# FFN gate and up as a seven-product block scheme, with the results kept in DRAM and the down products at the end

## The chip, the cores and the metric

The kernel runs on one core of one Trainium2 chip. The metric is the device time of one execution in microseconds (us), given as the median of three runs. The engines are TensorE (PE in the profile, with PEld for its weight loads), VectorE (DVE), ScalarE (ACT), GpSimd (POOL) and SyncE (SP), which here only issues DMAs. Each engine works through its own queue in order.

## The reference, cut to what matters

The input x is (16, 256, 512): 16 batches, 256 channels, 512 positions. The first half is a cross attention with 16 heads of 16 channels, whose queries come from the layer norm of x and whose keys and values come from `ctx`. The second half is an FFN over the last axis, with 1376 inner columns. Its weights are given as indices into a table of 16 values. All numbers are float32.

```python
x = x + xattn(layernorm(x), ctx, mask, mask, Wq, bq, Wk, bk, Wv, bv)

def ffn(x, lut, gate_idx, up_idx, down_idx):        # x: (16, 256, 512)
    gate = einsum('bsh,oh->bso', x, lut[gate_idx])  # (1376, 512) weights
    up   = einsum('bsh,oh->bso', x, lut[up_idx])
    h    = silu(gate) * up
    return einsum('bsh,oh->bso', h, lut[down_idx])  # (512, 1376) weights

x = x + ffn(layernorm(x), lut, gate_idx, up_idx, down_idx)
```

## The kernel before, in words

**Units of work.** The 16x256 rows of x make 32 row tiles of 128 rows by 512 columns, and four row tiles make a row block, so there are 8 blocks n = 0 to 7. The 1376 inner columns make 11 strips o of 128 columns (the last has 96). The 512 columns of x are four parts h of 128, the contraction steps of a matmul.

**Order.** The schedule is written out by hand (`tc.manual_schedule()`), so each engine's queue has the order in which the Python emits its instructions. The attention comes first, as 256 steps over (head group, key part). In each step TensorE makes the scores twice, in two layouts: `pa` (L458), which VectorE reduces to a row maximum (`nm`, L474, two reductions per step), and `pb` (L466), which ScalarE turns into exponentials (`pt`, L478). `pa` runs AHEAD = 7 steps before `pb`. The tables `lumps` and `after` hold what else is emitted at a step: projections, `apply_v`, sums, DMAs.

**Row tiles after the attention.** `finish_rows(k)` makes row tile k on GpSimd and SP stores it to DRAM (`x2_d[k]`, L554). Later `load_x2(k)` (L168) loads it, `stats2(k)` takes mean and variance on VectorE (`bn_f`, L98, L99), `rstd2` makes the reciprocal deviations (ScalarE square root L103, then VectorE L104, L105), `norm2(k)` (L181) normalizes, and `turn2(k)` transposes with four small matmuls (L192) and copies the result to `xT` with ScalarE (L193). For the first FIRST = 3 blocks this is done within the attention's last steps; for the later blocks it is done between the FFN's products (`preparing`).

**Weights.** Nothing is gathered: `look_up` turns a piece of indices into table values with 19 VectorE instructions (4 bits, L122 and L126; 8 leaves, L136; 7 joins by `copy_predicated`, L140). Gate and up (`wg`, `wu`) come in 32 pieces of 128x344; down (`wd`) comes in 11 pieces of 128x512. The first EARLY = 24 pieces are made during the attention, two instructions per step or one in a busy step. The others are made in the FFN by `fill`, which emits a given number of such instructions. SP loads the indices of a piece (`idx`, L634, and `idx_d`).

**The FFN.** `gate_up(n, o)` makes eight matmuls (four for gate, four for up, L715) of one block and strip into two PSUM banks of the pool `ps_a`, then ScalarE's silu (L720) and VectorE's product (`ht`, L722). `down(n)` makes, for each of four row tiles, 11 matmuls over the strips into one bank of `ps_b` (L731), adds the row tile (L736) and stores the output (L738). For blocks 0 to 2 all `gate_up` come first, strip by strip, with 11 `fill` instructions after each, and then three `down`; from block 3 on, each block has its 11 `gate_up`, with the next block's preparation between them, and then its `down`. The pool `ps_b` has four banks; `ps_a` has two buffers of two banks.

**SP.** SP issues all loads and stores of the attention's later steps and of the FFN in order. A store waits on SP for the engine that makes its data, and what is behind it waits as well.

A float32 matmul of the program is two records in the profile.

Of the kernel before, what the change touches and what calls it, by code (L numbers as in the profile page):

```python
# [19 lines left out]
def kernel(  # L20
# [88 lines left out]
    def look_up(pool, dst, it, name):  # L109


        rows, n = it.shape
        v = nc.vector

        def new(tag):
            return pool.tile([P, n], I32, tag=tag, name=f"{tag}_{name}")[:rows]

        m, ops = [], []

        def low():  # L120
            m.append(new("b0"))
            v.tensor_scalar(m[0], it, 31, 31, ALU.logical_shift_left, ALU.arith_shift_right)  # L122

        def bit(i):
            m.append(new(f"b{i}"))
            v.tensor_scalar(m[i], it, 1 << i, None, ALU.bitwise_and)  # L126

        ops.append(low)
        for i in range(1, 4):
            ops.append(lambda i=i: bit(i))  # L130
        d = dst.bitcast(I32)
        got = {}

        def leaf(k, to):
            a, c = lut_x[:rows, k : k + 1], lut_i[:rows, 2 * k : 2 * k + 1]
            v.tensor_scalar(to, m[0], a, c, ALU.bitwise_and, ALU.bitwise_xor)  # L136
            got[k] = to

        def join(level, k, k2):
            v.copy_predicated(got[k], m[level], got[k2])  # L140

        ops.append(lambda: leaf(0, d))
        ops.append(lambda: leaf(1, new("ta")))
        ops.append(lambda: join(1, 0, 1))
        ops.append(lambda: leaf(2, new("tb")))
        ops.append(lambda: leaf(3, new("ta")))
        ops.append(lambda: join(1, 2, 3))
        ops.append(lambda: join(2, 0, 2))
        ops.append(lambda: leaf(4, new("tb")))
        ops.append(lambda: leaf(5, new("ta")))  # L150
        ops.append(lambda: join(1, 4, 5))
        ops.append(lambda: leaf(6, new("tc")))
        ops.append(lambda: leaf(7, new("ta")))
        ops.append(lambda: join(1, 6, 7))
        ops.append(lambda: join(2, 4, 6))
        ops.append(lambda: join(3, 0, 4))
        return ops
# [4 lines left out]
    rstds = cpool.tile([P, NK], F32, tag="rstds", name="rstds")  # L162
    nmrs = cpool.tile([P, NK], F32, tag="nmrs", name="nmrs")
    x2s, xns = {}, {}

    def load_x2(k):
        x2s[k] = rpool.tile([P, T], F32, tag="x2", name=f"x2t_{k}", bufs=4)
# [17 lines left out]
    def turn2(k):  # L185
        n, t = divmod(k, 4)
        if t == 0:
            xTs[n] = xpool.tile([P, NH, 4 * P], F32, tag="xT", name=f"xT_{n}")
        pt = ps_b.tile([P, 512], F32, tag="b", name=f"pt_{k}")
        xn = xns.pop(k)  # L190
        for h in range(NH):
            nc.tensor.transpose(pt[:, h * P : (h + 1) * P], xn[:, h * P : (h + 1) * P], ident)  # L192
        nc.scalar.copy(xTs[n][:, :, t * P : (t + 1) * P], pt.rearrange("p (h r) -> p h r", r=P))  # L193


    with ExitStack() as att:
# [43 lines left out]
        def rstd1_of(lo, hi):  # L240
            at = slice(lo * NCC, hi * NCC)
            row_rstd(mv1[:, at, :], rstd1[:, at], nmr1[:, at])
# [366 lines left out]
                after[stats_at[b] - 3].append(lambda b=b: load_xs(b))  # L609
            after[stats_at[b]].append(lambda b=b: stats1(b))  # L610
        for lo, hi in ((1, 2), (2, 6), (6, B)):
            after[stats_at[hi - 1]].append(lambda lo=lo, hi=hi: rstd1_of(lo, hi))
        after[-8] += [fill_rows, lambda: (load_xs(1), load_b(1), load_piece(lp, 0))]
        after[-7].append(lambda: set_ones(0))
        after[-4].append(lambda: set_ones(1))
# [9 lines left out]
            for w, idx in ((wg, gate_idxT), (wu, up_idxT))  # L625
            for h in range(NH)
        ]
        EARLY = 24
        its = {}

        def load_piece(pool, i):
# [18 lines left out]
        early = lookups(lp, 0, EARLY)  # L650
        busy = {s for s in stats_at.values()} | {4 * u - 3 for u in range(NU)}

        NT = 4 * FIRST
        turns = NSTEP - 2 * NT
        for i in range(NT):
            after[turns - 5 - 3 * (NT - i)].append(lambda i=i: load_x2(i))
            after[turns - 3 - 3 * (NT - i)].append(lambda i=i: stats2(i))
            busy.add(turns - 3 - 3 * (NT - i))
            after[turns - 3 + 2 * i].append(lambda i=i: load_x2(i))
            after[turns + 2 * i].append(lambda i=i: norm2(i))  # L660
            lumps[turns + 1 + 2 * i].append(lambda i=i: turn2(i))
        after[turns - 4].append(lambda: rstd2(0, FIRST))
        for s in range(min(min(after), min(lumps)), NSTEP + 2):
            sa = s + AHEAD if 0 <= s + AHEAD < NSTEP else None
            sb = s if 0 <= s < NSTEP else None
# [4 lines left out]
            for fn in after.pop(s, ()):  # L670
                fn()
            if s >= 0:
                n = 0 if s in stats_at.values() else 1 if s in busy else 2
                for _ in range(n + (3 if sa is None else 0)):
                    next(early, None)
        for _ in early:
# [7 lines left out]
            last += after[s]  # L684


    with ExitStack() as ffn:
        wd_pool = ffn.enter_context(tc.tile_pool(name="wd", bufs=1))
        lp = ffn.enter_context(tc.tile_pool(name="lookup2", bufs=1))
        f1 = ffn.enter_context(tc.tile_pool(name="ffn1", bufs=1))  # L690

        wd = wd_pool.tile([P, NO, T], F32, tag="wd", name="wd")
        nblocks = NK // 4

        def rows_of(o):
            return min(P, INTER - o * P)

        def lookups_d():
            for o in range(NO):
                rows = rows_of(o)  # L700
                it = lp.tile([P, T], I32, tag="idx", name=f"idx_d{o}", bufs=2)
                nc.sync.dma_start(it[:rows], down_idxT[o * P : o * P + rows, :])
                for op in look_up(lp, wd[:rows, o, :], it[:rows], f"d{o}"):
                    op()
                    yield

        hts = {n: [] for n in range(nblocks)}

        def gate_up(n, o):
            rows = rows_of(o)  # L710
            at = slice(o * P, o * P + rows)
            ps = ps_a.tile([P, 2, 512], F32, tag="a", name=f"pgu_{n}_{o}")
# [5 lines left out]
                    )  # L718
            sg = rpool.tile([P, 4 * P], F32, tag="us0", name=f"sg_{n}_{o}", bufs=5)
            nc.scalar.activation(sg[:rows], ps[:rows, 0, :], AF.Silu)  # L720
            ht = f1.tile([P, 4 * P], F32, tag="ht", name=f"ht_{n}_{o}", bufs=FIRST * NO + 1)
            nc.vector.tensor_tensor(ht[:rows], sg[:rows], ps[:rows, 1, :], ALU.mult)  # L722
            hts[n].append((ht, rows))

        def down(n):
            hs = hts.pop(n)
            for t in range(4):
                xr = load_x2(4 * n + t)
                po = ps_b.tile([P, 512], F32, tag="b", name=f"po_{n}_{t}")
                for o, (ht, rows) in enumerate(hs):  # L730
                    nc.tensor.matmul(  # L731
                        po, ht[:rows, t * P : (t + 1) * P], wd[:rows, o, :],
                        start=(o == 0), stop=(o == NO - 1),
                    )
                ob = rpool.tile([P, T], F32, tag=("rb", "xr")[t % 2], name=f"ob_{n}_{t}", bufs=1)
                nc.vector.tensor_tensor(ob, po, xr, ALU.add)  # L736
                b, o = divmod(4 * n + t, NCC)
                nc.sync.dma_start(out[b, o * P : (o + 1) * P, :], ob)  # L738

        def preparing(n):  # L740

            k = 4 * n

            def at(i):
                if n >= nblocks:
                    return
                if i == 0:
                    for t in range(4):
                        load_x2(k + t)
                elif i == 1:  # L750
                    for t in range(4):
                        stats2(k + t)
                    rstd2(n, n + 1)
                    load_x2(k)
                elif i <= 9:
                    t = (i - 2) // 2
                    if i % 2:
                        turn2(k + t)
                    else:
                        norm2(k + t)  # L760
                        if t < 3:
                            load_x2(k + t + 1)

            return at

        late = lookups(lp, EARLY, len(pieces))
        late_d = lookups_d()

        def fill(n):
            for _ in range(n):  # L770
                if next(late, 1) == 1:
                    next(late_d, None)

        for o in range(NO):
            for n in range(FIRST):
                gate_up(n, o)
                if (o, n) == (0, 0):
                    for fn in last:
                        fn()
                fill(11)  # L780
        for _ in late:
            pass
        for _ in late_d:
            pass
        for n in range(FIRST):
            xTs.pop(n)
        prep = preparing(FIRST)
        for n in range(FIRST):
            down(n)
            for i in range(4 * n, 4 * n + 4):  # L790
                prep(i)
        for n in range(FIRST, nblocks):
            prep = preparing(n + 1)
            for o in range(NO):
                gate_up(n, o)
                prep(o)
            xTs.pop(n)
            down(n)


# [44 lines left out]
```

## Time and profile before

| | |
|---|---|
| median of 3 runs | 1978.93 us (1978.54 to 1982.69) |
| profiled execution, its time | 1980.16 us |
| profiled execution, its span | 1978.4 us |
| mean granted TensorE clock | 0.987 |
| PE busy | 1913.9 us (97%) |
| DVE busy | 1202.9 us (61%) |
| ACT busy | 767.9 us (39%) |
| POOL busy | 442.2 us (22%) |
| gate and up matmuls, L715 (two weights) | 318.5 + 316.5 us busy, 1408 records |
| down matmuls, L731 | 306.5 us busy, 704 records |
| first gate_up record | at 1029.07 us |
| end of the last down product | at 1974.36 us |

The span is the time from the first to the last instruction of the profiled execution. The page's groups give, for a line of the kernel, an engine and a tile, the busy time, the mean of one instruction in ns, and the idle time of the engine just before, with who ended it. The page's slices cut the span into 40 equal parts of 49.5 us. The chain of waits goes back from the last instruction to what released it at each step; it lists start, length, engine, tile and line. The timeline lists start, length, engine, line and operation, and in brackets the idle time before it and what ended that. `out<-in` names the tile written and the tiles read.

### The profile page before, as it was taken

The numbers are of one execution on the slowest core, as the hardware profiler recorded it, in microseconds if no ns is written. First come the engines' busy times: TensorE is split into PE (matmuls) and PEld (weight loads), VectorE is DVE, ScalarE is ACT, GpSimd is POOL, SyncE is SP. The second block draws the span as 40 slices with busy tenths as digits, with TensorE's granted clock in tenths as the row PEclk, the third lists the DMA queues.
The fourth block names the chain that finished last, engine by engine and source line by source line (L and its number), as shares of the span: only waits on it lengthen the run. The fifth ranks groups of instructions, "written<-read, shape, count | busy, mean of one in ns | idle before, by whom it ended". The sixth has DMA issues, their size and how long they took to land.

```text
span 1978.4 us, 23940 instructions
## 1 busy us (share of the span) xinstructions
PE 1913.9 (97%) x9030; PEld 788.8 (40%) x9030; DVE 1202.9 (61%) x1779; ACT 767.9 (39%) x1427; POOL 442.2 (22%) x511
## 2 busy tenths in 40 slices
PE   9999999999999999988998999989999999999999
PEld 4333333333333333333333444434444444444443
DVE  6898999999999998877996799710111101011000
ACT  2776776777777776656660000000110101011000
POOL 5444445444444444333320000000000000000000
PEclk9999999999999999989999999989999999999999
DMA  5454333443434434433321000021101001010101
GB/s 179 138 155 142 111 99 106 126 117 113 121 94 115 125 116 122 122 104 100 108 76 38 18 22 22 23 73 63 64 0 61 24 32 53 22 64 0 42 0 38
DMA packets 96676, 155.69 MB, mean 79 GB/s; under 512 B 20260, under 2 KB 25256, under 8 KB 96560
## 3 DMA queue, kind: packets, MB, share of 16 engines
q1 hardware_dynamic: 92288, 151.11, 25.2%
q0 software_dynamic: 3168, 1.86, 0.4%
q8 instruction: 71, 1.16, 0.2%
q10 hardware_dynamic: 1104, 1.19, 0.2%
q14 instruction: 45, 0.37, 0.1%
HBM read 113.29 MB, written 35.55 MB: 75 GB/s over the span
## 4 chain that ended last, share of the span: by engine, by line
PE 82%; DMA 5%; DVE 5%; ACT 3%; issue 2%; SPq 2%; POOL 1%; POOLq 0%; DVEq 0%; ACTq 0%
PE pgu L715 30%; PE po L731 15%; PE pa L458 12%; PE pv L497 9%; PE pb L466 7%; PE pv L422 3%; ACT pt L478 3%; PE pk L390 2%; PE pq L390 2%; DVE nm L474 2%; DMA x2t<-x 2%; DMA xs<-in_x_dram 1%; DMA qp<-qd 1%; DMA rb<-rd 1%; PE pt L192 1%
## 5 line engine op out<-in xcount | busy, mean ns | idle before, releaser
L474 DVE TENSOR_REDUCE nm<-pa 128x2 f32<-128x1024 f32 x512 | 601.9, 1217 | 74.8 <-PE pb L466 70.2
L478 ACT ACTIVATE pt<-pb 128x512 f32<-128x512 f32 x1024 | 530.8, 601 | 150.3 <-PE pb L466 145.9
L458 PE MATMUL pa<-kp,qp 32*128 32x512 f32 x2048 | 522.9, 623 | 20.5 <-DVE nm L474 17.7
L466 PE MATMUL pb<-qp,kp 32*128 32x512 f32 x2048 | 521.4, 624 | 0.1
L715 PE MATMUL pgu<-xT,wg 128*128 128x512 f32 (+1 forms) x704 | 318.5, 595 | 7.9 <-DVE ht L722 7.3
L715 PE MATMUL pgu<-xT,wu 128*128 128x512 f32 (+1 forms) x704 | 316.5, 592 | 0.0
L720 ACT ACTIVATE sg<-pgu 128x512 f32<-128x512 f32 (+1 forms) x88 | 52.5, 597 | 672.0 <-PE pgu L715 665.7
L731 PE MATMUL po<-wd,ht 128*128 128x512 f32 (+1 forms) x704 | 306.5, 597 | 0.0
L722 DVE TENSOR_TENSOR ht<-sg,pgu 128x512 f32<-128x512 f32 (+1 forms) x88 | 60.4, 686 | 350.5 <-ACT sg L720 350.4
L458 PEld LDWEIGHTS pa<-kp,qp 32*128 32x128 f32 x2048 | 182.1, 186 | 223.8 <-DVE nm L474 163.8
L497 PE MATMUL pv<-pt,va 128*32 128x512 f32 x2048 | 249.7, 606 | 2.3 <-ACT pt L478 2.3
L466 PEld LDWEIGHTS pb<-qp,kp 32*128 32x128 f32 x2048 | 202.1, 185 | 76.5 <-issue 49.1
L731 PEld LDWEIGHTS po<-wd,ht 128*128 128x128 f32 (+1 forms) x704 | 134.9, 192 | 169.6 <-issue 168.4
L715 PEld LDWEIGHTS pgu<-xT,wu 128*128 128x128 f32 (+1 forms) x704 | 132.0, 188 | 170.1 <-issue 170.1
L715 PEld LDWEIGHTS pgu<-xT,wg 128*128 128x128 f32 (+1 forms) x704 | 131.2, 188 | 171.7 <-issue 158.8
L736 DVE TENSOR_TENSOR ob<-po,x2t 128x512 f32<-128x512 f32 x32 | 22.1, 692 | 277.4 <-PE po L731 277.4
L497 PEld LDWEIGHTS pv<-pt,va 128*32 128x32 f32 x2048 | 54.3, 110 | 178.8 <-ACT pt L478 88.9
L502 ACT COPY us<-pv 128x512 f32<-128x512 f32 x128 | 75.0, 586 | 94.9 <-PE pv L497 94.9
L486 POOL DMA_DIRECT2D qp<-mx x64 | 38.5, 602 | 322.7 <-DVE mx L485 163.6
L509 POOL TENSOR_TENSOR us<-us,us 128x512 f32<-128x512 f32 x64 | 81.4, 1272 | 16.7 <-ACT us L502 16.6
L422 PE MATMUL pv<-wv,ctx 128*128 128x256 f32 x256 | 73.4, 411 | 7.6 <-ACT pt L478 0.4
L433 POOL TENSOR_SCALAR va<-vt,cols 128x128 f32<-128x128 f32 x128 | 76.0, 600 | 6.6
(108 smaller groups left out, 1254.4 us busy)
## 6 DMA issues: line engine op xcount, KB each, us to landing
x2t<-x SPq DMA_DIRECT2D x96, 256.0 KB
kp<-kd SPq DMA_DIRECT2D x62, 256.0 KB
qp<-qd SPq DMA_DIRECT2D x62, 256.0 KB
rb<-rd SPq DMA_DIRECT2D x32, 256.0 KB
xr<-in_x_dram SPq DMA_DIRECT2D x32, 256.0 KB
x<-xr SPq DMA_DIRECT2D x32, 256.0 KB
out_dram<-ob SPq DMA_DIRECT2D x32, 256.0 KB
kd<-natk SPq DMA_DIRECT2D x31, 256.0 KB
```

Of the source, the lines that this page charges most:

```text
L390: nc.tensor.matmul(ps, w[:, o, oc * P : (oc + 1) * P], src_t[:, o, :], start=(o == 0), stop=(o == NCC - 1),)
L422: nc.tensor.matmul(ps[:, :C], cx[:, o, c * P : (c + 1) * P], wv[:, o, :], start=(o == 0), stop=(o == NCC - 1),)
L433: nc.gpsimd.tensor_scalar(a4[:, e, :, 16 * e : 16 * e + 16], v4[:, e], m, None, ALU.mult)
L458: nc.tensor.matmul(pa[:, jj, :], qps[ua % 4][at, ca * P : (ca + 1) * P], kps[ua % 4][at, :], start=True, stop=True,)
L466: nc.tensor.matmul(pb, kps[ub % 4][at, cb * P : (cb + 1) * P], qps[ub % 4][at, :], start=True, stop=True,)
L474: nc.vector.tensor_reduce(nms[ua][:, 2 * half : 2 * half + 2, ca], pa, AX.X, ALU.max, negate=True)
L478: nc.scalar.activation(pts[sb][:, j, :], pb, AF.Exp)
L497: nc.tensor.matmul(ps[32 * j : 32 * j + 32, :], vas[b % 2][:, c, 8 * oc + 2 * j + e, :], pt[:, j, :], start=(i == 0), stop=(i == 1),)
L502: nc.scalar.copy(us[u, half], ps)
L509: nc.gpsimd.tensor_tensor(a, a, b, ALU.add)
L715: nc.tensor.matmul(ps[:rows, i, :], w[:, h, at], xTs[n][:, h, :], start=(h == 0), stop=(h == NH - 1),)
L731: nc.tensor.matmul(po, ht[:rows, t * P : (t + 1) * P], wd[:rows, o, :], start=(o == 0), stop=(o == NO - 1),)
```

## The change

**Seven products.** For two row blocks 2p and 2p+1 and one strip o, gate and up with both halves of the contraction form a product of two 2x2 block matrices: the weights are (a11 a12; a21 a22), with gate in the first row and up in the second and two parts h in each block; the activations are (b11 b12; b21 b22), with one column for each row block. The old way takes eight block products of two matmuls. The new `unit(p, o)` takes seven, by Winograd's form, and so needs sums of the weights (`combine_w`: S1, S2, S4 in the new tile `sw`, S3 in the place of a21) and of the activations (`combine_x`: the new tile `xe`, and T1 in the place of b12). Both are VectorE instructions, the sums of the weights of 512 to 768 elements per partition, those of the activations of 1024. Each product goes to one bank of `ps_b`. ScalarE copies the first; VectorE adds the others up with seven instructions that each read one PSUM bank; ScalarE makes silu twice; GpSimd multiplies twice; SP stores both results to DRAM (`hds`).

**Order of the FFN.** Strip 0 of blocks 0 to 3 is made by `gate_up` as before. Then come 42 units in the list `order`: strips 1 to 7 for the pairs 0 and 1 in turn, strips 8 to 10 of each of them, then pairs 2 and 3 with all 11 strips. A unit emits 14 `fill` instructions, between its adds. `hooks` puts the statistics of tiles 16 to 31 into units 0 to 8, one `rstd2` for all four later blocks into unit 9, and the normalizing and turning of blocks 4 and 5, and 6 and 7, into units 17 to 19 and 22 to 24.

**Down.** All eight `down` come after the last unit. The h of block 0 is loaded back at unit (3, 2); each `down(n)` first loads the row tiles and issues the load of block n+1 (2.8 MB, two buffers), whose memory is that of the sums and lookups, closed just before.

**Lookups.** EARLY is 22. Pieces 22 to 31 and the down weights are made in `between`, together with `combine_w`. Down pieces are halves of 256 columns, each with its own index load at its start.

**Attention.** Statistics are taken of 16 row tiles, not 12, and their loads stand four steps ahead, not two; `rstd2(0, 4)` stands two steps earlier. Block 3 is turned at the start of the FFN, into its own pool `x3pool` and through `ps_a`. `rstd1_of` of the later batches stands one step later. From step 179 on one lookup instruction is emitted per step, not two.

```diff
-        EARLY = 24
+        EARLY = 22
...
+        for i in range(16):
+            after[turns - 9 - 3 * (16 - i)].append(lambda i=i: load_x2(i))
+            after[turns - 5 - 3 * (16 - i)].append(lambda i=i: stats2(i))
...
-            after[turns - 5 - 3 * (NT - i)].append(lambda i=i: load_x2(i))
-            after[turns - 3 - 3 * (NT - i)].append(lambda i=i: stats2(i))
...
-        after[turns - 4].append(lambda: rstd2(0, FIRST))
+        after[turns - 6].append(lambda: rstd2(0, 4))
...
-                n = 0 if s in stats_at.values() else 1 if s in busy else 2
+                n = 0 if s in stats_at.values() else 1 if s in busy or s > turns - 54 else 2
...
+        def combine_w(lo, hi):
+            at = slice(lo, hi)
+            s1, s2, s4 = (sw[:, i, :, at] for i in range(3))
+            yield v.tensor_tensor(s1, a21[:, :, at], a22[:, :, at], ALU.add)
+            yield v.tensor_tensor(s2, s1, a11[:, :, at], ALU.subtract)
+            yield v.tensor_tensor(a21[:, :, at], a11[:, :, at], a21[:, :, at], ALU.subtract)
+            yield v.tensor_tensor(s4, a12[:, :, at], s2, ALU.subtract)
...
+            yield v.tensor_tensor(xe[:, 0], b22, b12, ALU.subtract)
+            yield v.tensor_tensor(b12, b12, b11, ALU.subtract)
+            yield v.tensor_tensor(xe[:, 1], b22, b12, ALU.subtract)
+            yield v.tensor_tensor(xe[:, 2], b21, xe[:, 1], ALU.subtract)
...
+        def unit(p, o, hooks):
...
+            def product(i, a, b):
+                ps = ps_b.tile([P, 512], F32, tag="b", name=f"p{i}_{p}_{o}")[:rows]
+                for h in range(2):
+                    nc.tensor.matmul(ps, a[:, h, at], b[:, h, :], start=h == 0, stop=h == 1)
+                return ps
...
+            nc.scalar.copy(p1, product(1, a11, b11))
...
+            add(w, product(6, sw[:, 1], xe[:, 1]), p1)
+            hooks[0]()
+            fill(2)
...
+            add(sg, product(2, a12, b21), p1)
+            nc.scalar.activation(sg, sg, AF.Silu)
+            fill(3)
...
+            add(r, product(7, a21, xe[:, 0]), w)
+            hooks[1]()
+            fill(2)
+            p5 = product(5, sw[:, 0], t1)
+            add(w, p5, w)
...
+            add(hb, p5, r)
+            fill(2)
...
+            add(ha, product(4, a22, xe[:, 2]), r)
+            nc.gpsimd.tensor_tensor(ha, ha, sg, ALU.mult)
+            store_h(2 * p, o, ha, rows)
+            hooks[2]()
+            fill(2)
+            add(w, product(3, sw[:, 2], b22), w)
+            nc.scalar.activation(w, w, AF.Silu)
+            nc.gpsimd.tensor_tensor(hb, hb, w, ALU.mult)
+            store_h(2 * p + 1, o, hb, rows)
+            fill(3)
...
         def down(n):
-            hs = hts.pop(n)
+            xrs = [load_x2(4 * n + t) for t in range(4)]
+            if n + 1 < nblocks:
+                load_h(n + 1)
...
+        for n in range(nblocks):
             down(n)
```

## The prediction

> **What bounds the kernel now.** I read the page first: its engines' shares, and the slices over time.
> ```profile
> PE 1913.9 (97%) x9030; PEld 788.8 (40%) x9030; DVE 1202.9 (61%) x1779; ACT 767.9 (39%) x1427; POOL 442.2 (22%) x511
> PE   9999999999999999988998999989999999999999
> DVE  6898999999999998877996799710111101011000
> PEclk9999999999999999989999999989999999999999
> ```
> TensorE is busy nearly throughout; VectorE is as full until slice 25, then nearly idle. Next I read the chain of waits from 950 us on.
> ```profile
> 1057.20 207.94 PE pgu L715 x480
> 1265.14 37.79 PE po L731 x88
> 1302.96 0.70 DVE ob L736
> 1304.59 3.25 DMA x2t<-x
> 1311.74 1.11 PE pt L192 x4
> 1442.82 13.74 PE pgu L715 x32
> 1456.55 0.44 PE pt L192 x4
> 1861.01 75.53 PE pgu L715 x176
> 1936.55 37.79 PE po L731 x88
> ```
> The FFN is matmul after matmul. 13.74 us for 32 records is 0.429 each, so a matmul (two records) takes 0.858, a 16-matmul gate-and-up of two row blocks 13.74, and a down product 37.78. Then the timeline around the attention's worst stall and the FFN's start, and after it two windows (start and end, length, then PE, PEld, DVE, ACT and POOL busy, clock, DMA).
> ```profile
> 867.56 0.69 DVE L98 BATCH_NORM_STATS2 bn_f<-x2t 128x6 f32<-128x512 f32 x1 [9.26 <-DMA x2t<-x]
> 1029.07 3.70 PE L715 MATMUL pgu<-xT,wg 128*128 128x512 f32 x8
> 1057.20 5.38 PE L715 MATMUL pgu<-xT,wg 128*128 128x512 f32 x8 [7.27 <-DVE ht L722]
> 1062.41 3.60 PE L715 MATMUL pgu<-xT,wu 128*128 128x512 f32 x8
> 1052.31 0.34 DVE L122 TENSOR_SCALAR b<-idx 128x344 int32<-128x344 int32 x1 [12.03 <-DMA idx<-in_L_ffn_gate_idx_dram]
> 843.18 1.26 POOL L509 TENSOR_TENSOR us<-us,us 128x512 f32<-128x512 f32 x1
> 843.39 1.46 DVE L140 COPY_PREDICATED tb<-b,tc 128x344 int32<-128x344 int32 x1
> ```
> ```profile
> 300.00:400.00 100.00, 99.06 (x708) 37.62 (x701) 92.61 (x114) 70.42 (x134) 45.78 (x51) 1.00 0.38 111
> 860.00:870.00 10.00, 2.40 (x13) 0.68 (x5) 2.41 (x5) 2.43 (x5) 2.77 (x3) 0.80 0.46 139
> ```
> Three things are to be seen. A load that SP issues late stops VectorE, and TensorE behind it (2.40 of 10 us busy, against 99.06 of 100). After such a pause the first eight records take 5.38 us, not 3.60: a stall costs 1.8 more. A lookup that meets a GpSimd instruction ends only after it (0.55 without).
>
> **What the change removes.** Now 42 units (four pairs of blocks, 11 strips, less two strips done the old way) take 14 matmuls each: 12.02 us, 1.72 less. That is 72 us of a bound engine. All eight down products stay at 37.78, or 302.3. The gaps around the first three of them (1302.96 to 1311.74, 1352.6 to 1359.1, 1397.9 to 1400.5: about 18 us) go, as statistics are no longer made there.
>
> **Attention.** The statistics of 16 row tiles, not 12, are taken here, their loads four steps ahead of use, not two; with 54 reductions per 100 us a step is 3.7 us, so 7.4 us more lead. From 760 to 950 us there are 90 reductions in 190 us; at 54.3 per 100 us they would take 166, so 24 us are lost. Of VectorE's idle there, 20 us waited for these loads, longest 9.26. The longest outlasts the new lead by 1.9; its place in the eight-step cycle comes twice among 16 loads, each with a 1.7 us slow clock. So I take 18 us gained. Bounds: 0, if the queue slips as much again; 24, if all goes. Two lookup pieces (38 instructions) leave, four statistics (0.85 each) come: VectorE has room. The first-layer rstd one step later: 0 to 2, taken as 0.
>
> **Start of the FFN.** From the last reduction (1004.4) VectorE needed 34.7 us to the first ht; the changed order has five instructions more, so 37.4, to 12.7 us after TensorE reaches the first gate_up (A). gate_up ends at A+6.9, the transposes of tiles 12 and 13 wait for VectorE and PSUM until A+14.9, and with a slow clock the second gate_up ends at A+23.5; tile 15 waits for its PSUM, then two more: A+39.4. Before, four took 36.8.
>
> **VectorE in a unit.** Seven adds at the ht spacing, 0.605: 4.24. Fourteen lookups: a 344-wide piece took 7.9 us net for 19, so 0.416 each, 5.8. The down weights now come in 256-wide halves (418 instructions for 209); carried on from 512 and 344 wide, about 0.35, 4.9 per unit. GpSimd multiplies twice per unit, 1.27 each, where it was idle. From 200 to 700 us lookups lost about 48 us (means 0.67 and 0.71 against 0.45 and 0.545) over 252 GpSimd instructions, 0.19 each; here lookups fill twice the share and the instruction is longer, so 0.7 each, 1.4 (0.4 to 2.55). That makes 11.4 us against TensorE's 12.02. Units 1 to 8 add two statistics, 1.65: 13.1. Combining 3x512 columns in units 1 and 2 replaces four lookups: 1.8 more (a 1024-wide reduction took 1.22; bounds 0.9 to 1.2 per 1024).
>
> The Trainium skill (SBUF — State Buffer, Who interferes with whom) says that the port pair shared with GpSimd is locked for a whole instruction, also against a VectorE instruction with two SBUF inputs, but not against one with a PSUM input. The trace shows it for lookups, and the reductions from PSUM stay at 1.217; no row shows two SBUF inputs. By it the combining would be held too, some 1 us in all.
>
> **What TensorE loses.** Four PSUM banks let it run three products (5.2 us) ahead of VectorE. At unit 0 VectorE is about 6.4 us behind, since piece 22's index load follows ht's store on SP (3.3) and four 1024-wide subtractions of x come first: 1.2. Units 0 to 8 need 118 on VectorE, 108.2 on TensorE: 9.8. The single rstd: 1. Twice, eight norms and a combine_x (8.5 together) sit in three units already near full: 5 each, and 16 transposes of 0.44, 7.0. In the down lookups an index load has no prefetch, and on SP it stands behind the store of the last h, which waits for GpSimd: add, silu 0.6, product 1.27, issues 0.9, landing 2.4 (as at 1049.82) make 5.3 us. While VectorE waits, its adds stand behind, and TensorE after its 5.2 us. By the changed order 8 of 21 pieces start behind a store (4.5 to 4.8), 3 shortly after (2.5), the rest not: 45 us over 28 units, 1.6 each. Then VectorE has 4.24+4.9+1.4+1.6=12.1, just TensorE's own, and I take 10 (0 to 30). The last half piece ends 13 us into the first down product, which wants it at 8.6: 4.4, and 1.8 for the clock. Together 38.4.
>
> **What stays hidden.** 88 stores and the reloads of h, 23 MB each way, against 253 GB/s reached in the first 20 us; a block of 2.8 MB has 37.8 us, and even at 100 GB/s takes 28. The first reload is issued about 13 us into the first product, so below 95 GB/s it would stall: some 6 us at 80. ACT gains a copy (0.59) per unit, 1.8 of 12. Row-tile loads stand behind h stores, but a unit ahead of use.
>
> **The sum.** FFN after: 39.4 + 42x12.02 (504.8) + 7.0 + 38.4 + 302.3 = 891.9; before 1029.07 to 1974.36 = 945.3. That is -53.4; with -18, -71.4. The profiled run took 1980.16 (span 1978.4, 1.76 around it): 1908.8. It lay 1.2 above the median 1978.93, so **1907**.
>
> **Rivals.**
> *The port lock at full length.* Each GpSimd product costs VectorE all of its 1.27: 1.15 more per unit, in 41 full units 47 us: 1954. For it: the 1.46 row lost nearly the whole. Against: the mean of 0.19.
> *TensorE's clock drops between products.* If bank waits of each of the 14 fullest units bring one half-rate spell (1.7): 24 us, 1931. Against: 300 to 400 us runs at 1.00 with such waits. The Trainium skill (TensorE: Matmul & The Clock Gate, the psum-queue depth-cycling section) tells of such a case; the trace speaks against it.
> *Slower: index loads hold VectorE.* The 12.03 row shows an index load stuck behind SP's queue that long. My mean is 2.1 over 21 pieces; at 6, 82 us more: 1989. It decides from 5.5 (72/21+2.1). Against: each store on the way needs only 5.3.
> *No loss in the units.* VectorE is lighter than I priced: the 9.8, the 10 and some of the turns go, the attention gains all: about 1876.
>
> **How the numbers follow.** My forecast 0.60, full lock 0.14, clock 0.06, index loads 0.08, no loss 0.12. The range 1870 to 1958 takes in no loss and the full lock and leaves out the index case and the far ends. Within 0.2% (4 us, about what these runs can tell) only a chance crossing lies: faster 0.91, same 0.01, slower 0.08.
>
> **What would show it.** Units of 12.0 us in the chain, 13 in the first nine, where "PE p <- DVE" waits appear; bn_f waits on x2t near zero before 950 us; idx_d waits of 4 to 5 us on VectorE; down products at 37.8 with no gap but the first; lookup means near 0.5 beside GpSimd. Wrong would be units over 13.7, idle before later down products, or an attention that ends no earlier.

## The result, and the profile after

| | before | after |
|---|---|---|
| median | 1980.32 us (1978.54 to 1982.69, 4 runs) | 1895.98 us (1895.19 to 1896.75, 4 runs) |
| profiled execution, time and span | 1980.16, 1978.4 us | 1895.36, 1893.5 us |
| first gate_up record (A) | 1029.07 us | 998.66 us |
| A to the last down product | 945.3 us | 891.2 us |

The ratio is 0.9573, 95% interval 0.9557 to 0.9590. The prediction was 1907 us (1870 to 1958): the direction was right, and the time 11 us lower. The FFN gained what was forecast (54.1 us, 53.4 predicted), the attention 30.4 us where 18 was forecast.

The engines' shares and the slices on the page of after answer those of before:

```profile
PE 1839.6 (97%) x8862; PEld 753.0 (40%) x8862; DVE 1439.6 (76%) x2226; ACT 779.6 (41%) x1457; POOL 557.5 (29%) x595
...
PE   8999999999999999999998899999999998999999
...
DVE  6999899999999999897897999979788885000000
...
PEclk9999999999999999999998999999999999999999
```

TensorE has 74 us less to do, and VectorE 237 us more, most of it in slices 27 to 34, where it stood nearly idle before. A slice of after is 47.3 us, so the slices of the two do not cover quite the same work. The attention's slices 18 and 19, 8s on TensorE before, are 9s. Behind the first slice, the 8s that after has are the start of the FFN (22 and 23) and the first down product (34).

Two rows of the windows view of after (start and end, length, PE, PEld, DVE, ACT and POOL busy, clock, DMA share, GB/s), and then one of before for the same stretch:

```profile
760.00:950.00 190.00, 185.06 (x1333) 72.14 (x1336) 164.02 (x209) 136.65 (x259) 77.44 (x87) 1.00 0.44 129
860.00:870.00 10.00, 10.00 (x80) 3.41 (x72) 8.56 (x10) 7.47 (x14) 5.93 (x7) 1.00 0.46 131
```

```profile
760.00:950.00 190.00, 171.59 (x1159) 63.80 (x1159) 150.47 (x206) 118.91 (x224) 71.60 (x81) 0.95 0.40 118
```

The ten microseconds from 860, in which TensorE was busy for 2.40 before, are full. No wait of `bn_f` for `x2t` is left in after; before had seven, 23.4 us.

Then the start of the FFN on TensorE in the timeline of after, and the end of its chain of waits:

```profile
998.66 3.70 PE L789 MATMUL pgu<-xT,wg 128*128 128x512 f32 x8
1002.20 3.60 PE L789 MATMUL pgu<-xT,wu 128*128 128x512 f32 x8
1011.29 1.11 PE L197 MATMUL pt<-ident,xn 128*128 128x128 f32 x4 [5.50 <-DVE xn L182]
1013.08 1.12 PE L197 MATMUL pt<-ident,xn 128*128 128x128 f32 x4 [0.68 <-ACT xT L198]
1013.99 5.82 PE L789 MATMUL pgu<-xT,wg 128*128 128x512 f32 x8
...
1038.64 1.88 PE L809 MATMUL p<-xT,wg 128*128 128x512 f32 x4
```

```profile
1395.41 163.69 PE p L809 x381
1559.10 7.67 issue
1566.79 1.33 POOL ha L836
1568.13 0.32 SPq L722
1568.56 1.98 DMA idx_d<-in_L_ffn_down_idx_dram
1570.56 0.29 DVE b_d L122
...
1584.02 2.21 DMA idx_d<-in_L_ffn_down_idx_dram
1586.26 0.29 DVE b_d L122
...
1593.20 296.66 PE po L949 x684
```

From 1395 to 1559 TensorE's 381 records follow one another at 0.430 us, so 28 records, a unit, take 12.03. The lines behind it are the mechanism that the prediction called the index loads: GpSimd's product of `ha` ends, SP issues its store and only then the load of the next `idx_d`, which lands 2 us later, and VectorE's lookups start. The last half piece repeats this, with its load at 1584.02. Its lookups end at 1593.16, and the first down product, begun at 1579.2, stands for these last weights until 1593.20.

### The profile page after: what moved, and what is told of

Same layout as the page of the kernel before. It is cut to its first block, busy times and chain, and to the rows that moved or that the text cites. A ratio compares the mean times of both kernels' runs of the same rounds, so it can differ in the third digit from the quotient of the medians.

```text
span 1893.5 us, 24623 instructions
## 1 busy us (share of the span) xinstructions
PE 1839.6 (97%) x8862; PEld 753.0 (40%) x8862; DVE 1439.6 (76%) x2226; ACT 779.6 (41%) x1457; POOL 557.5 (29%) x595
## 5 line engine op out<-in xcount | busy, mean ns | idle before, releaser
L949 PE MATMUL po<-wd,h 128*128 128x512 f32 (+1 forms) x704 | 305.4, 596 | 5.3 <-DVE wd L140 5.3
L949 PEld LDWEIGHTS po<-wd,h 128*128 128x128 f32 (+1 forms) x704 | 134.6, 191 | 175.9 <-issue 169.6
L809 PE MATMUL p<-xe,wu 128*128 128x512 f32 (+1 forms) x336 | 160.6, 601 | 9.0 <-DVE w L813 9.0
L836 POOL TENSOR_TENSOR ha<-ha,sg 128x512 f32<-128x512 f32 (+1 forms) x42 | 58.2, 1386 | 360.6 <-issue 313.4
L809 PE MATMUL p<-xT,sw 128*128 128x512 f32 (+1 forms) x336 | 159.6, 598 | 3.1 <-DVE sg L813 3.1
L809 PE MATMUL p<-xT,wg 128*128 128x512 f32 (+1 forms) x336 | 159.6, 598 | 0.0
L841 ACT ACTIVATE w<-w 128x512 f32<-128x512 f32 (+1 forms) x42 | 26.5, 630 | 279.8 <-DVE w L813 279.8
L491 POOL DMA_DIRECT2D qp<-mx x64 | 40.2, 628 | 294.4 <-DVE mx L490 141.5
L809 PEld LDWEIGHTS p<-xe,wu 128*128 128x128 f32 (+1 forms) x336 | 62.1, 188 | 95.0 <-issue 66.5
L809 PEld LDWEIGHTS p<-xT,wg 128*128 128x128 f32 (+1 forms) x336 | 63.0, 190 | 82.3 <-issue 70.1
L809 PEld LDWEIGHTS p<-xT,sw 128*128 128x128 f32 (+1 forms) x336 | 62.1, 188 | 79.8 <-issue 69.6
```

The source lines that it names most:

```text
L491: nc.gpsimd.dma_start(qps[u % 4][17 : P : 32, :].rearrange("j (c t) -> j c t", t=P), mx)
L809: nc.tensor.matmul(ps, a[:, h, at], b[:, h, :], start=h == 0, stop=h == 1)
L836: nc.gpsimd.tensor_tensor(ha, ha, sg, ALU.mult)
L841: nc.scalar.activation(w, w, AF.Silu)
L949: nc.tensor.matmul(po, hs[n][o][:rows, t * P : (t + 1) * P], wd[:rows, o, :], start=(o == 0), stop=(o == NO - 1),)
```

## The experiments

The ratio comes from all runs of a kernel; the other columns, times in us, come from its one profiled execution. "Units" is the time from the first record of unit 0 (of the first pair, in the run with eight products) to the first down record, "end" from there to the end of the span. Differences in us are made from the ratios to before, since the runs lie on several chips; after has 0.9573.

| run | ratio, 95% | A | A to unit 0 | units | end |
|---|---|---|---|---|---|
| after | 0.9573 (0.9557 to 0.9590) | 998.7 | 40.0 | 540.6 | 314.3 |
| loads two steps ahead | 0.9732 (0.9707 to 0.9756) | 1030.9 | 39.5 | 543.2 | 314.7 |
| rstd at its old step | 0.9595 (0.9567 to 0.9622) | 1008.4 | 39.7 | 543.7 | 314.3 |
| eight products | 0.9844 (0.9813 to 0.9876) | 999.9 | 40.1 | 602.6 | 306.1 |
| idx_d early | 0.9500 (0.9486 to 0.9514) | 998.9 | 40.1 | 528.7 | 310.3 |
| start in another order | 0.9529 (0.9515 to 0.9543) | 998.4 | 29.3 | 540.7 | 314.9 |
| both | 0.9456 (0.9442 to 0.9470) | 1000.0 | 29.3 | 531.5 | 310.4 |
| no GpSimd products | 0.9445 (0.9429 to 0.9461) | 1000.4 | 40.2 | 517.9 | 307.1 |
| both, products on VectorE | 0.9431 (0.9414 to 0.9448) | 1000.1 | 29.3 | 526.8 | 308.0 |
| both, no GpSimd products | 0.9378 (0.9363 to 0.9393) | 1002.7 | 29.3 | 518.2 | 307.1 |

### The attention: loads two steps ahead, in after

```diff
-            after[turns - 9 - 3 * (16 - i)].append(lambda i=i: load_x2(i))
+            after[turns - 7 - 3 * (16 - i)].append(lambda i=i: load_x2(i))
```

> The changed kernel with one edit: the loads of the 16 statistics tiles stand two steps ahead of their use, as in the kernel before, not four. Changed kernel: 1896.0 us, first gate_up record at 998.7. Theory A (of the 30.4 us by which the attention ends earlier, 26 come from the longer lead): the waits of bn_f on x2t come back, 15 to 25 us of VectorE idle, the first gate_up starts at 1017 to 1025, and the time is 1914 to 1922. Theory B (the gain is the lighter lookup load of the last 78 steps, the lead only hides what VectorE had room for anyway): the waits return in part, time below 1902.

Measured: 1931.1 us; the ratio is 0.0159 above that of after, or 31.5 us, more than theory A allowed and far from B. The waits of VectorE in this run, and then in before (what waited, what ended the wait; us in total, times, longest):

```profile
DVE bn_f L98 <- DMA x2t<-x: 29.9, 7, 6.2
```

```profile
DVE bn_f L98 <- DMA x2t<-x: 23.4, 7, 9.3
```

With 16 loads at the short lead VectorE waits 29.9 us for them; of before's 23.4, 3.3 lay in the FFN, so 12 loads cost 20.1. Theory A was sized by the 12. So the 31.5 us are what the longer lead is worth to 16 loads, and not a share of the 30.4 us by which the attention ends earlier.

### The attention: loads four steps ahead, in before

```diff
-            after[turns - 5 - 3 * (NT - i)].append(lambda i=i: load_x2(i))
+            after[turns - 7 - 3 * (NT - i)].append(lambda i=i: load_x2(i))
```

> The kernel before with one edit: the loads of its 12 statistics tiles stand four steps ahead of their use, not two. Kernel before: about 1980 us, first gate_up record at 1029.1. Theory A (the lead makes the attention's gain): VectorE's 20 us of waits on x2t before 950 us go, and the time falls to 1956 to 1964. Theory B (the lighter lookups of the changed kernel make it): 1974 to 1981, with the waits merely moved to other instructions.

Measured: 1961.86 us, ratio 0.9889 (0.9857 to 0.9921), 22 us less than before (16 to 28 by the interval); theory A. From the reductions of step 100 to those of the last step the profiled execution takes 577.0 us, where before takes 603.1, after 576.9 and the run above 608.2. So in these traces the edit is worth 26.1 us there, with no lighter lookups; after needs the same time with 16 loads and lighter lookups. This profile had lost 2.4 us to before by step 100, at a longer pause near 190 us (4.22 against 2.43).

### The attention: the rstd of the later batches

In after, put back:

```diff
-            after[stats_at[hi - 1] + (lo > 1)].append(lambda lo=lo, hi=hi: rstd1_of(lo, hi))
+            after[stats_at[hi - 1]].append(lambda lo=lo, hi=hi: rstd1_of(lo, hi))
```

> The changed kernel with one edit: rstd1_of of the later batches stands at its old step. Already at the 100th pair of reductions the changed kernel is 4.2 us ahead of the kernel before (394.9 against 399.1). Theory A (this edit makes these 4 us, as the square root no longer holds VectorE between statistics and reductions): the 100th pair is back at 399, time 1899 to 1901. Theory B (they come from elsewhere, and the step does nothing): 1895 to 1897.

Measured: 1902.91 us; the ratio is 0.0022 or 4.4 us above that of after, as in theory A, but the two intervals overlap. The profiled execution, 1907.99 us, was the longest of its four, so its A of 1008.4 in the table makes the edit look larger than the medians do. In before, the same line was moved in the change's direction, on top of the loads four steps ahead:

> Before, with only the two edits of the attention that need nothing of the FFN: the row tiles' loads four steps ahead of their use, and the first layer's rstd of the later batches one step later. It measures the attention's part of the gain by itself. The loads alone gave 22 us (ratio 0.9889); the rstd undone in after cost 4 us. Theory A (the two parts add, and the attention's part of the change is about 26 us, 8 more than the 18 predicted): ratio 0.985 to 0.988, first gate_up at 998 to 1002, and no TensorE spell at half rate near 67 and 190 us. Rival B (the rstd's step matters only with the changed kernel's order): ratio 0.988 to 0.990, first gate_up at 1004 to 1007.

Measured: 1960.91 us, ratio 0.9896 (0.9881 to 0.9911), the same as with the loads alone, and the first gate_up at 1008.0, later than either theory had it: rival B by the time. In the traces the step does something each time: at the old step TensorE pauses 2.43 to 4.22 us at about 190 us and a spell of the slow clock begins there (before, and both runs without the move), at the new one it pauses 1.81 us at most and there is none (after, this run and eight others). From the first reductions to those of step 100, after takes 377.5 us and before 382.0; from step 40 to 60, this run takes 78.3 and the one with the loads alone 81.9. But this run's profile then loses 4 to 5 us between steps 230 and 255, to after and to the loads alone. One place shows how. TensorE's timeline and the clock of the same stretch, first with the loads alone, then with both edits:

```profile
911.64 0.28 PE L483 MATMUL pmx<-ident,nm 128*16 128x128 f32 x1 [2.35 <-ACT pt L478]
912.13 1.13 PE L422 MATMUL pv<-wv,ctx 128*128 128x256 f32 x4 [0.21 <-ACT pt L478]
```

```profile
905.00:915.00 10.00, 7.44 (x61) 2.81 (x53) 7.32 (x12) 8.26 (x15) 4.43 (x5) 1.00 0.18 52
```

```profile
909.11 0.28 PE L483 MATMUL pmx<-ident,nm 128*16 128x128 f32 x1 [2.35 <-ACT pt L478]
909.60 1.91 PE L422 MATMUL pv<-wv,ctx 128*128 128x256 f32 x4 [0.21 <-ACT pt L478]
```

```profile
905.00:915.00 10.00, 7.44 (x45) 3.09 (x45) 5.92 (x12) 7.34 (x13) 4.25 (x6) 0.83 0.36 106
```

The pause is the same, 2.35 us, before the same instruction. Once the clock stays at 1.00, and the four records behind the pause take 1.13 us; once it is 0.83 over the ten microseconds, and they take 1.91. (The two windows begin 2.5 us apart in the work, so their counts of records do not compare.) A second spell follows at 937. So the traces show about 4 us gained by step 100, but whether the whole kernel keeps them is not settled: 4.4 us in after, nothing in before, and both intervals are wider than that.

### The FFN: eight products

After with two `gate_up` for each pair in place of a unit, and without the sums of weights and activations; order, stores, lookups and the attention stay.

```diff
-            unit(p, o, [lambda i=i, j=j: run(hooks.pop((i, j), ())) for j in range(3)])
+            gate_up(2 * p, o)
+            run(hooks.pop((i, 0), ()))
+            fill(7)
+            run(hooks.pop((i, 1), ()))
+            gate_up(2 * p + 1, o)
+            run(hooks.pop((i, 2), ()))
+            fill(7)
```

> The changed kernel with eight products in place of seven: each unit is two gate_up calls as in the kernel before (silu on ScalarE, product on VectorE), with the same 14 fill instructions, hooks, stores and order; no sums of weights or activations are made. Theory A (seven products save 72 us of TensorE, and the units lose about 29 of it again to VectorE): units of 13.73 us without stalls, 42 of them 577, with the transposes 584 against 540.6 in the changed kernel, so 1934 to 1946. Theory B (the loss in the units comes from GpSimd, stores or index loads and stays with eight products, too): 1896+72 = 1960 to 1970. Theory C (TensorE's matmuls were not the bound, VectorE's queue was): under 1920.

Measured: 1951.93 us, 53.8 us above after by the ratios. That lies between theories A and B: the seven products keep more of their 72 us than A had left, and less than B. By the table, 62.1 us lie in the units and 8.2 come back at the end: the eight products are slow enough for VectorE's last lookups, so the down products do not wait. The 10 us missing from 72 are the units' own losses: the units of after lose 28.7 us beyond 42 times 12.02 and 7.0 of transposes, the pairs here 18.6 beyond 42 times 13.74 and the same 7.0, all of it in the six pairs with transposes (17.7 to 19.4 us each).

The other reading of this run: from A to the end of the span it takes 948.8 us, before 949.3. So all else that changed in the FFN (the order, h through DRAM, all down products at the end) costs about as much as it gives. The change's gain is the attention's and that of the seven products.

### Index loads of the down pieces one piece earlier

```diff
                 to, it, name = its_d.pop(j)
+                ops = look_up(lp, to, it, name)
+                if j + 1 < 2 * NO:
+                    load_d(j + 1)
...
+            load_d(0)
```

> After, but the index load of each half piece of the down weights is issued one piece earlier (into a second buffer), so that no lookup waits for a load that has just been issued. It tests the term 'index loads in the down lookups': in after VectorE waited 44.8 us for idx_d in the units from 14 on (longest 6.5), the prediction had 45 us and took 10 us of it through to TensorE. Theory A (the wait costs TensorE only what the three products of lead do not cover): VectorE's waits for idx_d fall below 10 us; TensorE loses 6 to 14 us less: its idle time in units 17 to 27 (about 10 us in after) and the slow clock that follows it, the wait of the first down product (5.3) and its slow clock (3.4); time 0.3 to 0.7% below after, that is a ratio to before of 0.950 to 0.954 where after had 0.957. Rival B (VectorE is the bound of these units anyway, by the lookups themselves): the idle time goes to waits on sg or xe and the time falls by less than 3 us. Rival C (loads now collide with the stores of h on the queue): the waits stay above 25 us and the time does not move.

Measured: 1881.36 us, 14.5 us below after; theory A, at the upper end of its range or just beyond it. The waits for `idx_d` are gone, not only below 10 us. From the waits of VectorE in after, and of the same engine here:

```profile
DVE b_d L122 <- DMA idx_d<-in_L_ffn_down_idx_dram: 44.8, 14, 6.5
...
DVE w L813 <- PE p L809: 5.0, 9, 1.4
```

```profile
DVE w L823 <- PE p L819: 26.2, 37, 2.0
```

VectorE now waits for TensorE's products, 26.2 us in place of 5.0: it is ahead. Of 44.8 us of waits TensorE had felt 11.9 in the units and 3.9 at the end, where its wait in the first down product falls from 5.3 to 2.4.

### The start of the FFN in another order

```diff
+        while made[0] < 19 * EARLY - 24:
+            next(early)
+        norm2(NT)
+        norm2(NT + 1)
...
-        if n < FIRST:
+        if n < 4:
...
+        load_piece(lp, EARLY)
-        for fn in last:
-            fn()
...
+        for fn in last:
+            fn()
```

> After, with the start of the FFN in another order: tiles 12 and 13 are normalized before the last lookup instructions of the early pieces are out and not after them, tiles 12 to 15 are turned through the pool of four banks and not the one of two, and the index load of the next lookup piece is issued before the first store of h. It tests the term '39.4 us from the first gate_up to the first unit' and the 1.2 us stall of unit 0 (39.98 and 2.08 measured). Theory A (TensorE stands at this place because VectorE makes the norms late and the slow clock after the pause doubles the cost): the wait of 5.50 us for xn and the spell of 10.2 us at about 1008 shrink; first gate_up to first unit takes 28 to 32 us, the time falls by 6 to 11 us, a ratio to before of 0.951 to 0.954. Rival B (VectorE's work to the first ht sets it, whatever the order): the pause moves to a later tile, first gate_up to first unit stays at 37 or more, and the time falls by less than 3 us.

Measured: 1886.99 us, 8.7 us below after; theory A. TensorE's timeline of this run at the place shown above:

```profile
1001.90 3.60 PE L800 MATMUL pgu<-xT,wu 128*128 128x512 f32 x8
1005.33 1.04 PE L197 MATMUL pt<-ident,xn 128*128 128x128 f32 x8
1006.21 3.60 PE L800 MATMUL pgu<-xT,wg 128*128 128x512 f32 x8
...
1027.68 1.88 PE L820 MATMUL p<-xT,wg 128*128 128x512 f32 x4
```

No wait is left, and the second `gate_up` starts at full speed. The 39.4 us of the prediction were no necessity: 29.3 are four `gate_up` and their transposes. The stall of unit 0, which the early index load was to shorten, grew instead: TensorE comes there 10.7 us sooner, and the unit takes 16.9 us where it took 14.4.

### Both edits

> After with both edits: the index loads of the down pieces one piece earlier, and the start of the FFN in the other order. By theory A of both the gains lie in different places and add up: 14 to 22 us below after, a ratio to before of 0.946 to 0.950. If one takes the place of the other (VectorE carries what it saved at the start into the later units), the gain is no more than the larger of the two alone.

Measured: 1872.63 us, 23.2 us below after, a little more than expected, and the sum of 14.5 and 8.7: the gains add up in the time. In the table the units take 2.8 us longer than with the early loads alone: TensorE reaches them 10.8 us sooner, VectorE is not as much ahead, and a little of the start's gain is given back there.

### GpSimd's hold on VectorE

After without the two products on GpSimd:

```diff
-            nc.gpsimd.tensor_tensor(ha, ha, sg, ALU.mult)
...
-            nc.gpsimd.tensor_tensor(hb, hb, w, ALU.mult)
```

> After without the two GpSimd products per unit, so that h is not multiplied by up in blocks and strips made by units (that part of the reference is left out); stores and all other work stay. It tests the term 'GpSimd holds VectorE': 0.7 us taken for each of the two products in a unit. Theory A (a VectorE lookup that meets a GpSimd instruction ends only with it): the means of the 344-wide lookups at copy_predicated and tensor_scalar with two inputs fall from 0.67 and 0.57 to 0.55 and 0.45, those of the 256-wide ones from 0.54 and 0.51 to 0.45 and 0.41; units 3 to 8 fall from 12.3 to 13.8 to about 12.1, and VectorE's waits for idx_d get longer, not shorter, where it was not the bound; the stores come earlier as well, so idx_d waits of 4 to 6 us fall to 3 to 5; time 6 to 16 us below after, a ratio to before of 0.949 to 0.954. Rival B (the lookups are long for another reason, for example the form or the traffic of the stores): the means stay, units 3 to 8 stay above 12.8, and the time falls by less than 3 us.

Measured: 1869.45 us, 25.4 us below after, beyond theory A's range and far from B. Groups on VectorE from 1045 to 1230 us, in after and then here:

```profile
L136 DVE TENSOR_SCALAR ta<-b,lut_x,lut_b 128x344 int32<-128x344 int32 x38 | 22.0, 579 | 0.0
L813 DVE TENSOR_TENSOR w<-p,w 128x512 f32<-128x512 f32 x28 | 19.1, 682 | 0.0
L140 DVE COPY_PREDICATED tb<-b,ta 128x344 int32<-128x344 int32 x19 | 11.4, 601 | 0.4
...
L140 DVE COPY_PREDICATED tb<-b,tc 128x344 int32<-128x344 int32 x10 | 7.2, 725 | 0.2
```

```profile
L813 DVE TENSOR_TENSOR w<-p,w 128x512 f32<-128x512 f32 x30 | 20.5, 683 | 0.8 <-PE p L809 0.6
L136 DVE TENSOR_SCALAR ta<-b,lut_x,lut_b 128x344 int32<-128x344 int32 x38 | 17.1, 450 | 0.0
...
L140 DVE COPY_PREDICATED tb<-b,ta 128x344 int32<-128x344 int32 x19 | 10.3, 541 | 0.4
...
L140 DVE COPY_PREDICATED tb<-b,tc 128x344 int32<-128x344 int32 x10 | 5.4, 542 | 0.2
```

The lookups' means fall to 450 and 541 ns, the bare ones of 453 and 545 that before had after its attention, and the 256-wide ones to 405 and 444; the add that reads PSUM takes 682 and 683, so no hold on it shows. Units 3 to 8, from VectorE's first add to the next unit's, go from a mean of 12.98 us to 11.7: VectorE is behind at their start and now catches up. On TensorE they go from 12.65 to 12.02. Two things changed in this run: without GpSimd the stores leave earlier too, and the waits for `idx_d` fall from 44.8 to 17.8, not to the longer waits expected. So the same was tried on the version with both edits, where no load is late:

> The version with both edits and without the two GpSimd products per unit (the multiplication of silu(gate) by up is left out for what units make). It asks what is left of TensorE's losses when both named causes, the index loads and GpSimd's hold on VectorE, are gone. Theory A (these two were nearly all): first unit to first down product takes 512 to 516 us (42 units of 12.02 and 7.0 of transposes are 511.8), against 531.5 with the products; the down phase 302 to 304; time 15 to 22 us below the version with both edits, a ratio to before of 0.935 to 0.938. Rival B (VectorE's own work is too much in the turn blocks and with the statistics): 520 or more, and a ratio above 0.940.

Measured: 1857.7 us, 15.5 us below the version with both edits; theory A by the time. The units take 518.2 us, 6.4 above the bare 511.8 and a little above theory A's 516; the down products take 303.4, as it had them. The hold was thus worth about 15 us by itself, and of the 28.7 us that TensorE lost in the units 22.4 go with the two named causes. Of what is left, the waits are 3.3 in unit 0, where VectorE is just behind, and 1.0 for a `combine_x`.

Last, the products on VectorE, in the version with both edits:

```diff
-            nc.gpsimd.tensor_tensor(ha, ha, sg, ALU.mult)
+            v.tensor_tensor(ha, ha, sg, ALU.mult)
...
-            nc.gpsimd.tensor_tensor(hb, hb, w, ALU.mult)
-            store_h(2 * p + 1, o, hb, rows)
             fill(3)
+            v.tensor_tensor(hb, hb, w, ALU.mult)
+            store_h(2 * p + 1, o, hb, rows)
```

> The version with both edits (ratio to before 0.9456), but the two products of each unit, ha by sg and hb by w, made on VectorE and not on GpSimd. It asks whether GpSimd relieves VectorE at all. Rows: a 512-wide tensor_tensor of VectorE with two inputs in SBUF takes 0.605 from start to start (the sums of the weights), so two add 1.21 us per unit; in after the two GpSimd products cost VectorE 1.42 us per unit by the means of its 344-wide lookups and 1.14 by those of the 256-wide ones. Theory A (the lock costs nearly what the products would): the time stays within 4 us of that version, a ratio of 0.944 to 0.948, lookup means 0.45 and 0.54 (344 wide), units 3 to 8 near 12.2. Rival B (GpSimd still hides something: the second product waits for silu on ScalarE, and holds VectorE): 5 to 15 us slower. Rival C (the lock costs more than the means show): 5 to 12 us faster.

Measured: 1866.2 us, ratio 0.9431 (0.9414 to 0.9448), 5 us below the version with both edits, just beyond theory A and at the edge of C. The two intervals still touch, so it is at least not slower, and B is out. VectorE makes the two products itself, which the expectation priced at 1.21 us per unit, and loses nothing by it, since as much had been lost to the hold. Waits of TensorE from 990 us on, in the version with both edits and then here:

```profile
PE p L830 <- DVE w L834: 5.1, 7, 3.3
PE p L830 <- DVE sg L834: 3.7, 4, 1.9
PE po L969 <- DVE wd L140: 2.4, 1, 2.4
PE p L830 <- DVE xe L756: 2.0, 1, 2.0
```

```profile
PE p L830 <- DVE w L834: 3.6, 2, 3.3
PE p L830 <- DVE sg L834: 2.4, 2, 1.9
PE po L969 <- DVE wd L140: 1.7, 1, 1.7
PE p L830 <- DVE xe L756: 1.5, 1, 1.5
```

The mean clock of this execution is 1.000. The version beats both kernels: 115 us below before on the same chip (1981.24), and 28 below after by the ratios.

## Why the prediction was right, and where it was off

- **Seven products, 12.02 a unit, 72 us.** Right: undisturbed units take 12.02 to 12.03. Net of what VectorE and the end take back, 53.8 by the run with eight products.
- **Attention, 18 us for the loads (0 to 24).** The mechanism was right, and this is the term that was mis-sized: 26.1 in the traces, 22 by the time of before with this edit alone. The bound of 24 came from a window that ended at 950 us, but the stretch to the last step loses more (from step 240 to 255 before takes 56.2 us, after 53.0). And the two loads that I took to stay late did not: no `bn_f` waits for `x2t` in after.
- **The rstd one step later, 0 (0 to 2).** The traces show 4.4 us up to step 100. Together with the loads this makes the 30.4 of A, within 0.2, and that is 12 more than predicted; the time was missed by 11. How much of the rstd's part lasts is open.
- **Start of the FFN, 39.4.** 39.98. The slow clock was there as forecast: 5.82 us for eight records.
- **VectorE in units 1 to 8, 13.1 us; TensorE 9.8 behind in units 0 to 8.** From unit 0's first add to unit 9's are 117.7 us, 9.5 over nine times 12.02; units 3 to 8 have a mean of 12.98. Unit 0 stalled 2.08, not 1.2.
- **GpSimd's hold, 0.7 for each product.** With the bare durations of the run without products as base, lookups of after lost about 0.7 us per product up to unit 13 and about 0.6 in the down pieces. The rival of the lock at full length needed 1.27. The combining was held as well: see below.
- **Index loads, 45 us of waits, 10 felt by TensorE.** 44.8 and 11.9. The rival that ends slower needed a mean of 5.5 us over 21 pieces; measured are 2.1, the longest wait being 6.5. The 5.3 us that I gave a wait behind a store do not come out of the pieces named for it: these make 5.2 without the add and 5.8 with it.
- **Turn blocks, 5 and 5.** By VectorE's first adds, units 17 to 19 take 47.1 us and 22 to 24 take 43.4, where three bare ones of TensorE with their share of the transposes take 39.6: 7.5 (an index wait among them) and 3.8.
- **Last half piece, 4.4 and 1.8.** The wait was 5.3, and a spell of 6.8 us at half rate behind it costs 3.4.
- **Clock drops between products.** Three spells of 3.4 us in the units, about 5 us and not 24.
- **What stays hidden.** From the second down product on each takes 37.78, and no row has TensorE waiting for h. The first reload was issued 14.0 us into the first product, where I had 13.

The sum for the FFN, 891.9 against 891.2, is better than its parts, and this closeness is luck: the units lost 28.7 of the 32.0 taken for them, the start 0.6 and the end 2.1 us more than taken, and the losses listed in the prediction add up to 38.2, where its sum has 38.4.

## What to carry to other kernels

An engine that works beside the bound can be dear: moving two products from VectorE to GpSimd here relieved VectorE of nothing, because its lookups lost as much time to them; look at the means of the same instruction with and without the neighbour busy. Where one queue carries stores that wait for an engine and loads that another engine needs next, issue each load a piece ahead; here that gave 14.5 us. And a loss that is to be bounded by a window must be followed to the end of the stage, not to where the stalls look over.

## What the hardware showed that was not expected

A VectorE sum of two inputs in SBUF can be held by a GpSimd product as the lookups are. Timeline of after in unit 1:

```profile
1071.94 0.96 DVE L731 TENSOR_TENSOR sw<-wu 128x768 f32<-128x768 f32 x1
...
1072.19 1.83 POOL L842 TENSOR_TENSOR hb<-hb,w 128x512 f32<-128x512 f32 x1 [1.72 <-ACT w L841]
...
1072.93 1.91 DVE L732 TENSOR_TENSOR sw<-sw,wg 128x768 f32<-128x768 f32 x1
```

The second sum takes 1.91 us beside the product, and 0.957 in the version with the products on VectorE; the product itself, behind the first sum, takes 1.83 where its mean is 1.35. Either side may be the one that waits. The Trainium skill (SBUF — State Buffer, Who interferes with whom) states this rule; before had no row for it, and the trace agrees, as it does in that an add with one input in PSUM stays at 682 ns.

The slow clock does not follow from a pause's length alone: after the same idle 2.35 us of TensorE before the same instruction it came in one execution and not in the other. Between 70 and 74 us ten of the profiled executions share another pause, 2.30 us before the same four records. In eight no slow spell follows and the records take 1.98 us; in the two runs without GpSimd products, whose attention is the same program, the clock falls (0.66 from 71 to 76 us in one of them) and they take 3.39 and 2.47. The Trainium skill (TensorE: Matmul & The Clock Gate, HAM oscillation — how this bites in real kernels) sets the rule at gaps above about 3.4 us. Here shorter ones were enough in one case of two and in two of ten, so a forecast should price such a pause as a chance, not as a fixed 1.7 us.
